# The first 25 microseconds of a chain of eight blocks: statistics of row tiles in another order, one head instead of two corrected on TensorE, other filling products, another buffer

## The chip, the core and the metric

The kernel runs on one core of a Trainium2 chip. The metric is the device time of one execution, in microseconds (us); the number that counts is the median over runs. A core has TensorE (PE in the profile, its weight loads PEld), VectorE (DVE), ScalarE (ACT), GpSimd (POOL) and SyncE (SP), which issues the DMAs here. Each has its own in-order queue of instructions, and they wait for each other by semaphores. Matrix products write to eight banks of PSUM, 128 partitions by 512 numbers each; all else lies in SBUF.

## The reference

x has shape (2, 512, 512): two sequences b of 512 rows, in float32. Eight blocks follow each other, and each adds its result to x:

```
x = x + attn_a(layernorm(x))      # latent attention, 32 heads      <- the change is in here
x = x + ffn(layernorm(x))         # dense layer with adapters
x = x + attn_b(layernorm(x))      # grouped-query attention
x = x + ffn(layernorm(x))
x = x + attn_mla(...); + experts(...); + attn_mha(...); + experts(...)
```

The first block, cut to what matters (`X` is the normalised x, b one sequence):

```
C_q  = X @ Wq_d + bq_d            # 512 x 12
C_kv = X @ Wkv_d + bkv_d          # 512 x 4: keys and, through Wv_u, values of all heads
q    = C_q @ W_qk + b_qk          # 32 heads of width 4
attn = softmax(q_h @ C_kv.T / 2)  # per head
out  = concat_h(attn @ V_h) @ Wo + bo,   V = C_kv @ Wv_u + bv_u
```

## The kernel before, in words

**Tiles.** The 1024 rows of x are eight row tiles t of 128 (`NT` = 4 of each sequence). A layernorm of a tile is `statistics` (three VectorE instructions: L205, L207, and L241 inside `inv_sqrt`, whose power is a GpSimd instruction, L243), then `centred` (L215 on VectorE: subtract the mean, multiply) into one of two buffers "xn", then `place` (four transposes on TensorE, L228, and a ScalarE copy to `xT`, L233).

**High and low halves.** The first block does its score products in the type float32r, whose products are cheap and keep fewer bits. To lose nothing, queries, keys and weights each lie several times along the partitions, some copies as the full number rounded (high) and some as what rounding left over (low). `halved` makes this with two instructions of one engine: `high` = full times a mask (L481), which rounds, and then full plus `high` (L482). The mask of a partition is -1 where the low part is wanted and 0 elsewhere. Its temporary comes from the tag "high", a ring of two buffers.

**A head's queries.** The kernel groups the 32 heads of a sequence into eight products, called `head(b, t)` here, t = 0 to 7 (one 128x512 product each, L503). There are two ways to get their halves:
- by TensorE: ScalarE copies the product to `high` (L506), a second product with `rest` (the masked identity) subtracts it in PSUM (`correct`, L199), and ScalarE copies the result to `qs` (L509). Heads 0 and 1 of the first sequence go this way;
- by GpSimd: ScalarE copies the product to the buffer "wv_diag" (L513; this tag has one buffer), and GpSimd halves it (L481, L482). The others go this way.

**The opening** (L769 to L793) is written out by hand for TensorE and VectorE (`manual_schedule` on both: their instructions keep the order of the code; the order on ScalarE, GpSimd and SyncE is left to the scheduler). `warm(n)` issues n transposes of the identity whose result nobody reads (L86). Then, in order: 30 of these; row tiles 0 to 3 in pairs (statistics of two tiles, centring of the two, and for each tile `place` and 5 or 10 identity products); GpSimd's `fills`, held back behind the last power; the halves of the weights `wqks` (L784, L785); the statistics of row tiles 4 to 7; `queries(0)` (eight product instructions, L473; then L497 and the halves on VectorE) and `latents(0)` (eight more L473; then L490 and the halves, which give `keys`); then heads 0 and 1 side by side, with `fill(2)` after each of three rounds. `fill(n, bank)` issues n products of `unit` (the identity) with `keys[0]`, also read by nobody (L755); unlike those of `warm` they need the keys. The rounds are: both heads' products and L506; both corrections and L509; nothing.

**Twelve steps** follow (L804 to L812). Here only TensorE's order is the code's. Each step has two score products on 32 rows (L589, each read by a VectorE maximum, L597), a slice of other work taken from the list `extra` (`slices(1)`: one piece of cost 1), and `fill(2)`. The list holds, in order: centring of tiles 4 and 5, heads 2 and 3, placements of tiles 4 and 5, centring of 6 and 7, values of the latents (L521, L525), head 4, placements of 6 and 7, heads 5, 6, 7. Eight steps are one unit of scores u; unit u needs head u. After the eighth step the adapters' coefficients are computed on VectorE (L848 to L859), after the ninth `maxima(0)` (four transposes, L615, a correction, L199, and a ScalarE copy, L618) makes the operands of the transposed scores.

**The main loop** has 16 units of eight steps; a step has two scores, two transposed scores (L627, in three banks in turn, each read by an exponent on ScalarE, L630), and a slice of other work or eight value products (L637). The second sequence's projections and heads are done in these slices. Everything behind the first block is scheduled in its own sections, with TensorE's order as written.

**Banks.** From L781 to the main loop, `k.turn()` hands out the banks 3, 4, 5, 7 in turn; scores have 0, 1, 2, and bank 6 takes the filling products.

Of the kernel before, what the change touches and what calls it, by code (L numbers as in the profile page):

```python
# [32 lines left out]
F32R = mybir.dt.float32r  # L33
# [7 lines left out]
NT = S // P  # L41
KC = D // P
NTILES = B * NT
# [385 lines left out]
def attn_latent_small(k, a):  # L429
# [8 lines left out]
    nc, tc = k.nc, k.tc  # L438
    with ExitStack() as ctx:
        lp = ctx.enter_context(tc.tile_pool(name="a", bufs=2))  # L440
# [18 lines left out]
        keys = [one([P, S], f"keys{b}", F32R) for b in range(B)]  # L459
# [4 lines left out]
        def fills():  # L464
            nc.gpsimd.tensor_scalar(rest, k.ident, low[:, 1:2], 1.0, ALU.mult, ALU.mult)
            nc.gpsimd.memset(nm[0], 0.0)
            nc.gpsimd.tensor_copy(unit, k.ident)
            for t in (nm[1], *vals):
                nc.gpsimd.memset(t, 0.0)

        def chained(ps, pairs):
            for i, (lhsT, rhs) in enumerate(pairs):
                nc.tensor.matmul(ps, lhsT, rhs, start=(i == 0), stop=(i == len(pairs) - 1))  # L473
                yield 1

        def halved(engine, out, full, at, tag="high"):

            top = lp.tile(list(out.shape), F32R, tag=tag, name="high")  # L480
            engine.tensor_scalar(top, full, low[:, at : at + 1], 1.0, ALU.mult, ALU.mult)  # L481
            return engine.tensor_tensor(out, full, top.bitcast(F32), ALU.add).ins  # L482

# [2 lines left out]
        def latents(b):  # L486
            ps = k.turn()
            yield from chained(ps, [(wkvd[:, c], k.xT[b][:, c]) for c in range(KC)])
            full = fulls[b] = one([P, S], "full")
            nc.vector.tensor_scalar(full, ps, bkvc, None, ALU.add)  # L490
            k.latest = halved(nc.gpsimd if b else nc.vector, keys[b], full, 0)

        def queries(b):
            ps = k.turn()
            yield from chained(ps, [(wqd[:, c], k.xT[b][:, c]) for c in range(KC)])
            full = one([P, S], "full")
            nc.vector.tensor_scalar(full, ps, bqd, 0.5, ALU.add, ALU.mult)  # L497
            cqs[b] = one([P, S], "cq", F32R)
            halved(nc.gpsimd if b else nc.vector, cqs[b], full, 2)

        def head(b, t):
            ps = k.turn()
            nc.tensor.matmul(ps, wqks[:, t], cqs[b], start=True, stop=True)  # L503
            if (b, t) < (0, 2):
                top = lp.tile([P, S], F32R, tag="high", name="high")
                nc.scalar.copy(top, ps)  # L506
                yield 1
                k.correct(ps, rest, top)
                nc.scalar.copy(qs[b][:, t], ps)  # L509
                yield 0  # L510
                return
            full = one([P, S], "wv_diag")
            nc.scalar.copy(full, ps)  # L513
            halved(nc.gpsimd, qs[b][:, t], full, 1)
            yield 1

        def latent_values(b):

            tp = k.turn()
            for t in range(NT):  # L520
                nc.tensor.transpose(tp[:, bass.ts(t, P)], fulls[b][:, bass.ts(t, P)], k.ident)  # L521
            part = tp.rearrange("p (t d) -> p t d", t=NT)[:, :, 0:5]
            for i in range(4):
                to = vals[b][:, :, i, 5 * i : 5 * i + 5]
                k.latest = nc.vector.tensor_copy(to, part).ins  # L525
            yield 1
# [3 lines left out]
        def centre(*ts, bias=None):  # L530
            for t in ts:
                normal[t] = k.centred(t, bias and bias(), known.pop(t, None))
            yield 0

        def put(t, back=False):
            k.place(t, normal.pop(t), k.turn, back)
            yield 1
# [42 lines left out]
        of_values, other = 6, (7,)  # L580
# [167 lines left out]
        def run(pieces):  # L748
            for piece in pieces:
                for _ in piece:  # L750
                    pass

        def fill(n, bank):
            for _ in range(n):
                nc.tensor.matmul(k.held[:, bank], unit, keys[0], start=True, stop=True)  # L755
# [13 lines left out]
        k.ring = k.EVERY  # L769
        with tc.manual_schedule(engines={mybir.EngineType.PE, mybir.EngineType.DVE}):  # L770
            k.warm(30)
            for t in range(0, NT, 2):
                pair = [k.statistics(t + i) for i in range(2)]
                centred = [k.centred(t + i, known=pair[i]) for i in range(2)]
                for i in range(2):
                    k.place(t + i, centred[i], k.turn)
                    k.warm(5 + 5 * i)
            with tc.issue_after(k.root):
                fills()
                k.masks()  # L780
            k.ring = (3, 4, 5, 7)  # L781
            wqks = k.w.tile([P, 8, P], F32R, tag="w8", name="wqks", bufs=5)
            top = k.w.tile([P, 8, P], F32R, tag="w8", name="high", bufs=5)
            nc.vector.tensor_scalar(top, wqk, low[:, 3:4], 1.0, ALU.mult, ALU.mult)  # L784
            nc.vector.tensor_tensor(wqks, wqk, top.bitcast(F32), ALU.add)  # L785
            known = {t: k.statistics(t) for t in range(NT, NTILES)}
            run([queries(0), latents(0)])
            first = k.latest
            starts = [head(0, t) for t in range(2)]
            for _ in range(3):  # L790
                for piece in starts:
                    next(piece, None)
                fill(2, of_values)  # L793
        extra = [centre(NT, NT + 1), head(0, 2), head(0, 3), put(NT), put(NT + 1)]
        extra += [centre(NT + 2, NT + 3), latent_values(0), head(0, 4), put(NT + 2)]
        extra += [put(NT + 3), head(0, 5), head(0, 6), head(0, 7)]

        later = [queries(1), latents(1)] + [head(1, t) for t in range(4)] + [latent_values(1)]
        later += [fold_bias()] + [head(1, t) for t in range(4, 8)] + [fold()]
        later += [add(t) for t in range(NTILES)]  # L800

        behind = []
        with tc.manual_schedule(engines={mybir.EngineType.PE}):
# [10 lines left out]
            extra = later  # L814
# [871 lines left out]
class Experts:  # L1686
# [111 lines left out]
    def bias(self):  # L1798
        return self.k.load_row(self.a["f1_bias"], D, "bias")
# [370 lines left out]
@with_exitstack  # L2170
def kernel(ctx: ExitStack, tc: tile.TileContext, a: dict, out: bass.AP):
    k = Block(ctx, tc, a["x"], out)
    k.hold()
    block = attn_latent_small(k, a)
    bound = CausalBound(k, a)
    attn_gqa(k, a, bound, block)
    ffn_lora(k, a, block)
    attn_mla(k, a)
    k.release(ctx)
    with k.tc.tile_pool(name="f1", bufs=2) as own:  # L2180
        experts = Experts(k, a, own)
        with k.tc.tile_pool(name="heads", bufs=1) as pool:
            rooms = HeadRooms(k, a, pool)
            experts.first(rooms.fill)
            attn_mha(k, a, bound.register(), rooms, experts)
        experts.end()
# [168 lines left out]
```

## Time and profile before

| | |
|---|---|
| median of three runs | 1966.16 us |
| the three runs | 1965.16 to 1968.29 us |
| the profiled execution: its own time | 1967.16 us |
| its span in the trace | 1965.4 us |
| granted TensorE clock | 0.997 |
| PE, DVE, POOL, ACT busy | 98%, 70%, 52%, 48% of the span |
| instructions of PE | 15610 |

The profile comes from one execution. Line numbers (L503) are those of the code above. In the chain of work that ended last each line is a start, a length and the engine and line that the end hung on at that time. In a timeline each line is a start, a length, an engine, a line, output<-input, sizes and a count; in brackets stands how long the engine was idle before and what ended that. A matrix product's start and end are modelled, so that neighbouring products overlap a little in the timeline, while the chain gives each its own share.

### The profile page before, as it was taken

The numbers are of one execution on the slowest core, as the hardware profiler recorded it, in microseconds if no ns is written. First come the engines' busy times: TensorE is split into PE (matmuls) and PEld (weight loads), VectorE is DVE, ScalarE is ACT, GpSimd is POOL, SyncE is SP. The second block draws the span as 40 slices with busy tenths as digits, with TensorE's granted clock in tenths as the row PEclk, the third lists the DMA queues.
The fourth block names the chain that finished last, engine by engine and source line by source line (L and its number), as shares of the span: only waits on it lengthen the run. The fifth ranks groups of instructions, "written<-read, shape, count | busy, mean of one in ns | idle before, by whom it ended". The sixth has DMA issues, their size and how long they took to land.

```text
span 1965.4 us, 40501 instructions
## 1 busy us (share of the span) xinstructions
PE 1927.3 (98%) x15610; PEld 1198.6 (61%) x15610; DVE 1374.7 (70%) x3457; ACT 938.1 (48%) x2460; POOL 1020.1 (52%) x1112
## 2 busy tenths in 40 slices
PE   9989999999999999999999999999999999999999
PEld 5333356777777777777777545666565554654654
DVE  8889658767776676777775577777677755847853
ACT  3876624444444343444443167666666411641550
POOL 4331055776756667677763246565655546216221
PEclk9999999999999999999999999999999999999999
DMA  3010212323322322232223213020101002002001
GB/s 136 17 44 1 76 66 64 86 73 88 96 67 57 97 77 81 76 98 76 79 79 85 72 22 109 7 74 7 62 13 55 23 12 48 2 3 43 2 2 44
DMA packets 69296, 108.96 MB, mean 55 GB/s; under 512 B 13922, under 2 KB 48994, under 8 KB 62052
## 3 DMA queue, kind: packets, MB, share of 16 engines
q1 hardware_dynamic: 68804, 104.15, 18.2%
q8 instruction: 127, 2.08, 0.4%
q0 software_dynamic: 288, 2.10, 0.3%
q14 instruction: 77, 0.63, 0.1%
HBM read 80.00 MB, written 4.19 MB: 43 GB/s over the span
## 4 chain that ended last, share of the span: by engine, by line
PE 86%; POOL 5%; DVE 5%; issue 3%; ACT 1%; SPq 1%; DMA 0%; POOLq 0%; DVEq 0%; ACTq 0%
PE held L1004 13%; PE held L281 11%; PE held L1139 9%; PE held L190 9%; PE held L357 8%; PE held L637 3%; PE held L589 3%; PE held L1076 3%; PE held L473 2%; PE held L1498 2%; PE sc L190 2%; PE held L1495 1%; PE tp L1771 1%; DVE nm L597 1%; PE held L1496 1%
## 5 line engine op out<-in xcount | busy, mean ns | idle before, releaser
L302 ACT ACTIVATE room<-room,nmax 128x128 f32<-128x128 f32 (+3 forms) x384 | 212.6, 557 | 354.5 <-DVE nmax L292 352.2
L281 PE MATMUL held<-kT,q 128*32 128x32 f32 (+15 forms) x4096 | 263.8, 397 | 5.3 <-DVE invs L310 1.7
L292 DVE CUSTOM_DVE_ANT_0 room<-held,mask 128x128 f32<-128x128 f32 (+3 forms) x384 | 179.1, 488 | 63.3 <-PE held L281 57.7
L281 PEld LDWEIGHTS held<-kT,q 128*32 128x32 f32 x4096 | 143.3, 110 | 87.0 <-issue 37.7
L357 PE MATMUL held<-turned,vals 32*128 32x384 f32 (+7 forms) x2784 | 189.7, 416 | 1.5 <-issue 1.5
L597 DVE TENSOR_REDUCE nm<-held 128x1 f32<-128x512 f32 x256 | 161.6, 683 | 23.3 <-PE held L627 17.9
L357 PEld LDWEIGHTS held<-turned,vals 32*128 32x128 f32 (+1 forms) x2784 | 149.2, 167 | 40.3 <-issue 23.8
L315 ACT ACTIVATE room<-room,invs 128x128 f32<-128x128 f32 (+3 forms) x316 | 153.3, 551 | 41.8 <-DVE invs L310 41.7
L254 DVE TENSOR_TENSOR rows<-rows,held 128x512 f32<-128x512 f32 x198 | 129.5, 673 | 31.9 <-PE held L1004 31.3
L330 DVE STREAM_TRANSPOSE turned<-room 128x1152 f32<-128x1152 f32 x80 | 107.8, 1361 | 40.7 <-ACT room L315 21.6
L243 POOL TENSOR_TENSOR rstd<-ve,mhalf 128x1 f32<-128x1 f32 x64 | 36.3, 569 | 179.2 <-DVE ve L241 176.0
L1165 POOL TENSOR_TENSOR q<-q,room 128x256 f32<-128x256 f32 x64 | 45.2, 728 | 123.7 <-DVE q L1148 113.0
L1183 POOL TENSOR_TENSOR q<-q,cosq 128x512 f32<-128x512 f32 x60 | 88.0, 1467 | 31.6 <-DVE t L1180 31.6
L1139 PE MATMUL held<-room,w 128*128 128x256 f32 x384 | 95.0, 383 | 0.0
L1184 POOL TENSOR_TENSOR q<-q,t 128x512 f32<-128x512 f32 x64 | 86.7, 1355 | 6.3 <-DVE q L1183 2.5
L302 ACT ACTIVATE probs<-probs,nmax 128x128 f32<-128x128 f32 (+3 forms) x128 | 70.6, 553 | 37.4 <-DVE nmax L292 36.6
L589 PEld LDWEIGHTS held<-keys,qs 32*128 32x128 f32 x256 | 30.9, 181 | 94.2 <-DVE nm L597 67.0
L1004 PE MATMUL held<-w,ctxT 128*128 128x256 f32 x360 | 86.5, 383 | 0.1
L630 ACT ACTIVATE pt<-held 128x512 f32<-128x512 f32 x128 | 69.7, 599 | 29.8 <-PE held L627 26.8
L630 ACT ACTIVATE room<-held 128x512 f32<-128x512 f32 x128 | 69.8, 599 | 26.7 <-PE held L627 22.1
L589 PE MATMUL held<-keys,qs 32*128 32x512 f32 x256 | 76.9, 494 | 5.5 <-DVE nm L597 5.2
L2105 POOL TENSOR_SCALAR_AFFINE_SELECT room<-room 128x512 f32<-128x512 f32 x32 | 20.3, 635 | 119.0 <-ACT room L2101 119.0
(439 smaller groups left out, 5011.9 us busy)
## 6 DMA issues: line engine op xcount, KB each, us to landing
w<-in_b_wq SPq DMA_DIRECT2D x16, 1024.0 KB, 4.9
w<-in_b_wo SPq DMA_DIRECT2D x16, 1024.0 KB, 5.3
vals<-v SPq DMA_DIRECT2D x256, 64.0 KB, 2.1
w<-in_m_wo SPq DMA_DIRECT2D x8, 1024.0 KB, 6.6
w<-in_b_wk SPq DMA_DIRECT2D x16, 256.0 KB, 2.7
w<-in_b_wupv SPq DMA_DIRECT2D x16, 256.0 KB, 2.6
w<-in_m_wqn SPq DMA_DIRECT2D x8, 384.0 KB, 3.6
rows<-in_x SPq DMA_DIRECT2D x8, 256.0 KB, 4.2
```

The source lines that it names most:

```text
L190: last = self.nc.tensor.matmul(out, lhsT, rhs, start=(i == 0), stop=(i == len(pairs) - 1))
L254: self.nc.vector.tensor_tensor(x, x, ps.rearrange("p (t d) -> p t d", t=2), op)
L281: nc.tensor.matmul(ps[32 * i : 32 * i + 32, a - lo : b - lo], q[:, at : at + 32], keys[:, a:b], start=True, stop=True,)
L292: nc.vector.tensor_tensor_reduce(out=row, in0=ps[:, :kv], in1=self.mask_back[:, :kv] if qt % 2 else self.mask[:, S - kv :], op0=ALU.add, o ...
L302: nc.scalar.activation(row, row, AF.Exp, bias=nmax, scale=-1.0, accum_out=total[:, qt : qt + 1])
L315: self.nc.scalar.activation(row, row, AF.Identity, scale=each)
L357: self.nc.tensor.matmul(out[:, :, :n], values(i, j), rhs, start=(j == blocks[0]), stop=(j == stop[i]),)
L589: nc.tensor.matmul(ps, qs[b][rows[g], 4 * half + i, bass.ts(qt, P)], keys[b][rows[g]], start=True, stop=True,)
L597: k.latest = nc.vector.tensor_reduce(nm[u % 2][:, qt, at : at + 1], ps, AX.X, ALU.max, negate=True).ins
L630: nc.scalar.activation(probs[u, kc][:, g], ps, AF.Exp)
L1004: k.nc.tensor.matmul(out, lhsT[:, i, bass.ts(t, P)], rhs[i], start=not (after or t or i), stop=i == 1, skip_group_check=True,)
L1139: nc.tensor.matmul(out, lhsT[:, c], rhs[:, c], start=c == 0, stop=c == 1)
```

## The change

- In the order of VectorE, the statistics of tile 2 come before the centring of tile 0, and those of tile 3 between the centrings of 1 and 2. The order on TensorE of placements and identity products stays.
- The statistics of tile 7 come behind `queries(0)` and its halves, ahead of those of `latents(0)`.
- The temporary of the keys' halving of the first sequence is a buffer of the tag "wv_diag" and no longer one of "high".
- Only head 0 is corrected on TensorE in the opening. Head 1 becomes a piece of `extra`, ahead of head 2, and is halved by GpSimd.
- Between head 0's parts stand two times five identity products (`warm`) where there were filling products with the keys; one `fill(2)` remains of three.

```diff
-            top = lp.tile(list(out.shape), F32R, tag=tag, name="high")
+            top = lp.tile(list(out.shape), F32R, tag=tag, name="high", bufs=1 if tag != "high" else None)
...
-            k.latest = halved(nc.gpsimd if b else nc.vector, keys[b], full, 0)
+            k.latest = halved(nc.gpsimd if b else nc.vector, keys[b], full, 0, "high" if b else "wv_diag")
...
-            if (b, t) < (0, 2):
+            if (b, t) == (0, 0):
...
             k.warm(30)
-            for t in range(0, NT, 2):
-                pair = [k.statistics(t + i) for i in range(2)]
-                centred = [k.centred(t + i, known=pair[i]) for i in range(2)]
-                for i in range(2):
-                    k.place(t + i, centred[i], k.turn)
-                    k.warm(5 + 5 * i)
+            ahead = [k.statistics(t) for t in range(3)]
+            centred = [k.centred(t, known=ahead[t]) for t in range(2)]
+            ahead.append(k.statistics(3))
+            for t in range(NT):
+                if t == 2:
+                    centred += [k.centred(i, known=ahead[i]) for i in (2, 3)]
+                k.place(t, centred[t], k.turn)
+                k.warm(10 if t % 2 else 5)
...
-            known = {t: k.statistics(t) for t in range(NT, NTILES)}
-            run([queries(0), latents(0)])
+            known = {t: k.statistics(t) for t in range(NT, NTILES - 1)}
+            run([queries(0)])
+            known[NTILES - 1] = k.statistics(NTILES - 1)
+            run([latents(0)])
             first = k.latest
-            starts = [head(0, t) for t in range(2)]
-            for _ in range(3):
-                for piece in starts:
-                    next(piece, None)
-                fill(2, of_values)
-        extra = [centre(NT, NT + 1), head(0, 2), head(0, 3), put(NT), put(NT + 1)]
+            for _ in head(0, 0):
+                k.warm(5)
+            fill(2, of_values)
+        extra = [centre(NT, NT + 1), head(0, 1), head(0, 2), head(0, 3), put(NT), put(NT + 1)]
```

## The prediction, made before the changed kernel ran

> **What bounds the kernel now.** I read the page's busy shares first: PE is busy for 98% of the span, so the time is the time of TensorE's queue, and an edit counts by how much earlier or later that queue gets through. Then I read the chain that ended last over the stretch which the change touches, the first 45 us (columns: start, length, what):
>
> ```profile
> 10.03 1.08 DVE xn L215
> ...
> 11.16 0.65 PE held L228 x4
> 11.81 1.09 PE held L86 x10
> 12.91 6.88 PE held L473 x16
> 19.82 0.76 DVE full L490
> 20.60 0.50 DVE high L481
> 21.12 0.70 DVE keys L482
> 21.82 0.14 issue
> 21.96 0.70 PE held L755 x2
> 22.66 0.46 PE held L199 x2
> 23.12 0.91 PE held L755 x4
> 24.02 0.43 PE held L589 x2
> ```
>
> The reader is to see three sections: row tiles up to 12.91, two projections (L473) up to 19.8, then the keys' tail on VectorE and, behind it, 2.06 us of PE products (21.96 to 24.02) before the first scores (L589). None of those products but the corrections (L199) computes anything.
>
> Third, the table of busy time by stretches (length, then busy time of PE, weight loads, VectorE, ScalarE, GpSimd):
>
> ```profile
> 19.80:24.00 4.20, 2.48 (x12) 1.47 (x11) 2.85 (x5) 2.25 (x4) 0.00 (x0) 1.00 0.85 302
> 24.00:42.70 18.70, 18.16 (x81) 9.94 (x80) 16.82 (x37) 5.77 (x11) 10.09 (x12) 1.00 0.01 1
> ```
>
> PE is idle only in the first; in the second, VectorE is nearly as full as PE. Last, ScalarE in order of time, at two places:
>
> ```profile
> 21.91 0.59 ACT L506 CAST high<-held 128x512 fp32r<-128x512 f32 x1 [1.27 <-DVE keys L482]
> ...
> 42.94 0.59 ACT L513 COPY wv_diag<-held 128x512 f32<-128x512 f32 x1 [2.19 <-POOL qs L482]
> 43.42 1.10 ACT L630 ACTIVATE room<-held 128x512 f32<-128x512 f32 x2
> ```
>
> The first is head 1's high half waiting for a buffer that the keys' halving reads. The second is a ScalarE copy waiting for GpSimd with the first exponent (L630) right behind it: this is where the gain may be lost again.
>
> **Part 1, statistics of three tiles first.** Nothing is added or taken away: eight tiles' statistics, eight centrings. One tile's statistics are 1.02 us of VectorE (those of tile 0 start at 3.54, those of tile 1 at 4.56). The third tile's now stand before tile 0's centring, so that moves from 5.56 to 6.58, ends at 7.12, and PE's first transposes (L228) start at 7.18 instead of 6.16. The last centring gains: statistics 3 now end near 8.7, its GpSimd power (0.55 to 0.81) near 9.55, so tile 3 is centred by 10.15 (0.55, as the unhindered rows) to 10.65 (1.07, as this one took beside GpSimd's fills), against 11.10. But PE's queue is a list of its own: four placements at 0.59 and 30 identity products at 0.109 (10 in 1.09) are 2.36 + 3.27 = 5.63 us without a gap. 7.18 + 0.06 + 5.63 = 12.87. The projections start at 12.87 instead of 12.91: I take **-0.03 us**. Bounds: if the identity products did not stand in the way, tile 3 at 10.15 plus 0.06 + 0.59 + 1.09 gives 11.9, -1.0; if row tile 2 lands late, tile 0 waits for it. Landings took 2.7 to 4.4 us from issue, tile 2 is issued near 1.7, so 4.4 to 6.1 against a need at 5.58: up to +0.5. The median of the first four, 2.9, says 4.6, in time.
>
> **Part 2, statistics 7 behind the queries' halves.** The queries' L497 waited until 17.01 behind four statistics although its products end near 16.35. It now starts there. Its result is needed by the first head product, behind the keys' products at 19.79, and was ready at 19.0 already: **0**, hidden by L473. The moved statistics (1.02) fit between the queries' halves (end 18.3) and the keys' L490 at 19.8. With that slack of 1.5 gone they would push the keys back by up to 1.02.
>
> **Part 3, head 1 taken out of the opening, another buffer for the keys.** Before: keys at 21.82, then 0.14 issue, 0.70 for two products, 0.46 for two corrections, 0.91 for four products: scores at 24.02. After: head 0's product, five identity products, its correction near 20.66 (head 0's high half ends at 20.63 in this trace and waits for nothing), five identity products, its copy ready near 21.5, all before the keys; then 0.14 + 0.70 and the scores. The corrections (0.46) and four products (0.91) leave the path: **-1.37 us**. The ten identity products are 1.09 us inside the gap in which PE now idles (1.72 before L755): 0. Head 1's L506 wait goes with it. First scores: 24.02 - 0.03 - 1.37 = 22.62. What is late next there is the keys' tail itself (L490 to L482, 1.96 us), unchanged.
>
> A rule to weigh here. The row: the first 30 identity transposes alone ran 15 in the 3.0 us from 1.5 and 17 in the 1.8 us from 4.5, 0.20 against 0.11 us each. The Trainium skill (TensorE: Matmul & The Clock Gate, Part 4: PE-mode transpose) says that transposes do not count as PE work for the clock gate in the way products do; by it the new filling would leave PE looking idle from 19.8 to 21.9, still shorter than the page's window of about 3.4 us (Part 1). By the page's worst reading the next 3.4 us would run at half speed, an estimate of +1.7 us. The row speaks against the reading (transposes alone got the speed up), and I add nothing.
>
> **Part 4, head 1 comes back in the loop.** Twelve steps (two scores, a slice, two filling products), 24.02 to 42.70, 18.68 us. PE's own work there: 12 x (0.43 + 0.46) = 10.68, six heads at 0.43 = 2.58, four placements 2.36, latent values 0.60, maxima 0.68: 16.90; the other 1.78 is waiting for VectorE. The twelfth step had an empty slice; now twelve slices hold seven heads, +0.43. VectorE's work is 24 reductions at 0.62, two centrings 1.00, 0.43 of value copies, 1.71 of adapter coefficients: 18.0, so it is about equally late, and part of the +0.43 falls into PE's waits (38.80 to 41.48 is all VectorE in the chain). Bounds 0 to +0.43; I take **+0.2**, the nearer row being that VectorE stretch in the very last steps. The first step of the main loop then starts at 42.70 - 1.40 + 0.2 = 41.5.
>
> On GpSimd and ScalarE head 1 costs a copy (0.59), L481 (0.70) and L482 (1.27), one more turn of a chain that repeats every 2.76 us (copies at 24.92 and 27.68), since "wv_diag" is one buffer. Heads 1 to 3 end near 31.8 instead of 30.4, head 4 near 34.5, before the split of maxima near 35.3 (36.67 now): no wait. Head 2 is needed only in the main loop.
>
> **Sum.** -0.03 - 1.37 + 0.2 = **-1.2 us**, if nothing later gives it back; from 42.7 on the loop is PE's (56.94 busy of 57.30 up to 100 us) and moves as a whole. The profiled execution took 1967.16 (span 1965.4 and 1.76 around it), so 1965.96 on its own time; it lay 1.0 above the median of 1966.16, and against that median I forecast **1965.0**.
>
> **Rivals.**
>
> *ScalarE's queue gives it back (slower than before).* Heads 5, 6, 7 move one step later each: head 5's product from 36.69 to about 37.5. Their copies go through the single buffer, so head 7's copy ends 0.67 + 5.58 + 0.59 later, at 44.3, while the first exponents are ready near 41.9 now. If they stand behind that copy in ScalarE's queue, the first ends at 44.8 instead of 44.0, and the fourth transposed score of the main loop, which needs the first of three banks, comes at 44.9 against 44.3: +0.5 over before, so -1.2 turns into **+0.5: 1966.7**. It decides as soon as head 7's copy is placed ahead of the first L630. For it: that is the order of the rows above, and the copy waited 2.19 there. Against: at 42.94 the copy was ready before the exponents (43.1), now it is ready 1.4 us after them, and ScalarE's order is not written out by hand; VectorE's centrings at 21.73 ran ahead of reductions that stand before them in the code.
>
> *The rest of the program is ordered anew.* Outside the opening only TensorE has a fixed order. A stall as at 100.11 to 104.70 (copy, GpSimd halves, VectorE, 1.7 us of PE idle in that stretch) may appear or vanish; three of them are 5 us, to **1971** or, vanishing elsewhere as well, **1961**. Nothing in the profile points to either.
>
> *The reordering does nothing at all:* with keys' tail and PE list as they are, parts 1 and 2 give 0 in any case; if part 3's products are only replaced by a wait for head 0's copy (23.45 now), scores start near 23.6: **1965.9**.
>
> **How the numbers follow.** About 0.2% (3.9 us, 1962.2 to 1970.1) is what a measurement of this kernel can tell from no change. Chances: forecast 0.50, ScalarE's queue 0.23, nothing but part of it 0.09: all within it, 0.82. New order for the worse 0.09, for the better 0.09. The range takes the first three, the bounds of part 1 (-1.0, +0.5) and of part 4, and about 1 us by which the three runs shown lie apart on either side: 1962.2 to 1968.2.
>
> **What would show it.** The changed profile should have the first L473 at 12.87, the keys at 21.8, first scores at 22.6, one L506 and no wait of ScalarE for the keys; L513 fifteen times for fourteen. The first L627 near 41.6 says part 4 is right; the order of the last L513 and the first L630 behind 41 us decides between forecast and first rival. I am wrong if the projections start before 12.4 (then the identity products did not bound), if tile 2's landing ends VectorE's wait, or if the difference arises after 100 us.

## The result and the profile after

The changed kernel takes 1972.04 us (median of 22 runs, 1965.50 to 1975.44) against 1966.32 us before (22 runs beside it): a ratio of 1.0028, 95% interval 1.0022 to 1.0034. It is slower by some 5.5 us; 1965.0 had been forecast, with 1968.2 as the upper end.

The profiled execution took 1972.26 us, with a span of 1970.5. Its chain of work that ended last, at the place shown of before and on to the main loop (start, length, what):

```profile
7.11 0.66 PE held L228 x4
...
12.35 6.88 PE held L473 x16
...
20.57 0.70 DVE keys L482
21.27 0.14 issue
21.40 0.70 PE held L755 x2
22.10 0.42 PE held L589 x2
...
41.19 0.70 POOL high L481
41.89 0.07 issue
41.96 1.27 POOL qs L482
43.23 0.02 issue
43.25 0.59 ACT wv_diag L513
43.85 0.04 issue
43.89 0.79 PE held L627
44.68 2.01 PE held L473 x2
46.69 0.72 PE held L589 x2
```

Two things are to be seen. Up to 22.10 the change does more than was forecast: the first scores come 1.92 us earlier than before (24.02); about 0.5 of that lies within what executions differ by (see the run with the statistics alone). But between 41 and 43.9 the chain no longer runs through TensorE. It runs through GpSimd's halves of head 6 and ScalarE's copy of head 7 (L513), and behind them a pair of projection products takes 2.01 us. In the chain of before such a pair (L473 x2, from 43.30) takes 1.05.

TensorE's queue at that point, in order of time (the bracket is the idle time before an instruction and what ended it), and ScalarE's:

```profile
40.59 0.50 PE L589 MATMUL held<-keys,qs 32*128 32x512 f32 x2
41.14 0.49 PE L627 MATMUL held<-qm,keys 32*128 32x512 f32 x1
43.89 0.79 PE L627 MATMUL held<-qm,keys 32*128 32x512 f32 x1 [2.26 <-ACT wv_diag L513]
44.61 2.08 PE L473 MATMUL held<-room,w 128*128 128x512 f32 x2
```

```profile
40.50 0.59 ACT L513 COPY wv_diag<-held 128x512 f32<-128x512 f32 x1 [2.19 <-POOL qs L482]
43.25 0.59 ACT L513 COPY wv_diag<-held 128x512 f32<-128x512 f32 x1 [2.16 <-POOL qs L482]
43.74 0.60 ACT L630 ACTIVATE room<-held 128x512 f32<-128x512 f32 x1
```

The first transposed score (L627) runs on time. The second one waits 2.26 us, and what releases it is the copy of head 7's product. In the kernel before the first two ran together and the projections followed at once:

```profile
42.80 0.50 PE L627 MATMUL held<-qm,keys 32*128 32x512 f32 x2
43.23 1.12 PE L473 MATMUL held<-room,w 128*128 128x512 f32 x2
```

The second score and head 7's product have a PSUM bank in common. The ring of banks 3, 4, 5, 7 is advanced by every turn, and the two calls of `warm` take a turn each. So head 7's product lies in bank 5 now (it lay in bank 3 before), and bank 5 is the second of the transposed scores' three.

How TensorE's clock went meanwhile, in the table of busy time (length, busy time of PE, weight loads, VectorE, ScalarE, GpSimd, then the granted clock, DMA share and rate):

```profile
41.00:42.00 1.00, 0.58 (x3) 0.18 (x1) 0.97 (x3) 0.09 (x1) 0.73 (x2) 1.00 0.00 0
42.00:43.00 1.00, 0.00 (x0) 0.00 (x0) 0.41 (x1) 0.00 (x0) 1.00 (x1) 0.90 0.00 0
43.00:44.00 1.00, 0.11 (x1) 0.11 (x1) 0.00 (x0) 0.75 (x2) 0.28 (x2) 0.50 0.00 0
44.00:50.00 6.00, 6.00 (x13) 1.76 (x13) 1.29 (x2) 2.02 (x4) 1.89 (x2) 0.50 0.00 0
50.00:56.00 6.00, 6.00 (x20) 1.78 (x20) 3.58 (x6) 2.46 (x5) 0.58 (x3) 0.50 0.02 4
56.00:57.00 1.00, 1.00 (x12) 0.03 (x4) 1.00 (x2) 0.80 (x2) 0.92 (x2) 0.77 0.84 250
```

The seventh number of each line falls from 1.00 to 0.50 while TensorE stands idle, and it stays there for 13.65 us (42.80 to 56.46), though TensorE is busy all the time from 43.9 on. In this execution that is most of the loss. At a place in the code that both kernels reach (the first transposition at L655) the profile after is 6.6 us late, 147.6 against 141.0. At the last block's projections it is 4.7 us late (1582.9 against 1578.2), mostly because the execution profiled of before had a half clock of 3.4 us near 1160 us that this one did not have; it accounts for 1.7 of the 1.9 us between the two.

**Taking the clock apart from the waits.** Every run lists its mean granted clock. Time x (1 - clock) is how much of TensorE's clock was withheld, and the rest of the time is a figure for the program at full clock. It is a reckoning and not a measurement of its own: it also counts clock that is withheld while TensorE waits (in the profile after, 42.80 to 43.89), so it puts a little of a wait down to the clock. Averaged over the runs:

| kernel | median, us | ratio to before, 95% | withheld clock, us | at full clock, us |
|---|---|---|---|---|
| before (35 runs beside the first four) | 1966.35 | | 5.2 | 1960.8 |
| changed | 1972.04 | 1.0028 (1.0022 to 1.0034) | 9.3 | 1962.35 |
| warm products in bank 6 | 1968.60 | 1.0016 (1.0007 to 1.0026) | 8.2 | 1961.0 |
| ten filling products more | 1968.69 | 1.0014 (1.0005 to 1.0023) | 6.2 | 1962.2 |
| heads 5 and 6 earlier | 1969.05 | 1.0017 (1.0007 to 1.0027) | 8.9 | 1960.4 |
| before, statistics alone | 1966.25 | 0.9999 (0.9990 to 1.0008) | 5.1 | 1960.9 |
| changed, copies in buffers of their own | 1964.40 | 0.9990 (0.9981 to 0.9999) | 5.9 | 1958.4 |
| changed, two heads on TensorE | 1965.77 | 0.9996 (0.9987 to 1.0005) | 6.4 | 1959.45 |
| before, head 7 in bank 5 | 1967.03 | 1.0000 (0.9992 to 1.0009) | 4.5 | 1961.6 |
| changed, no warm products | 1973.53 | 1.0040 (1.0025 to 1.0055) | 12.6 | 1960.9 |
| before, copies in buffers of their own | 1963.92 | 0.9990 (0.9981 to 0.9999) | 3.9 | 1960.1 |
| as the copies' one, no warm products | 1966.55 | 1.0001 (0.9990 to 1.0013) | 8.2 | 1958.1 |

The runs were taken in three groups, each with runs of before beside it, to which its ratios refer: rows 3 to 6 (before as in the first row), rows 7 to 10 (before 1966.50, 5.8 withheld, 1960.7 at full clock) and the last two (1965.08, 4.9, 1960.8). The changed kernel's ratio refers to the 22 runs of before beside it, whose clocks are not on record. The standard errors of the last two columns are 0.1 to 0.4 at full clock and 0.3 to 0.7 for the clock (1.2 and 1.7 in the two runs without warm products). The changed kernel's 5.6 us over the first row, by these means, are 4.1 of clock and 1.5 of waits.

### The profile page after: what moved, and what is told of

Same layout as the page of the kernel before. It is cut to its first block, busy times and chain, and to the rows that moved or that the text cites. A ratio compares the mean times of both kernels' runs of the same rounds, so it can differ in the third digit from the quotient of the medians.

```text
span 1970.5 us, 40514 instructions
## 1 busy us (share of the span) xinstructions
PE 1932.3 (98%) x15615; PEld 1199.2 (61%) x15615; DVE 1374.8 (70%) x3457; ACT 937.2 (48%) x2459; POOL 1023.5 (52%) x1114
## 4 chain that ended last, share of the span: by engine, by line
PE 87%; POOL 5%; DVE 5%; issue 2%; ACT 1%; DMA 0%; SPq 0%; DVEq 0%; POOLq 0%; ACTq 0%
PE held L1006 13%; PE held L281 11%; PE held L1141 9%; PE held L190 9%; PE held L357 8%; PE held L637 3%; PE held L589 3%; PE held L1078 3%; PE held L473 2%; PE sc L190 2%; PE held L1500 2%; PE held L1497 1%; PE pj L190 1%; PE tp L1773 1%; PE held L1498 1%
## 5 line engine op out<-in xcount | busy, mean ns | idle before, releaser
L315 ACT ACTIVATE room<-room,invs 128x128 f32<-128x128 f32 (+3 forms) x316 | 153.3, 551 | 41.6 <-DVE invs L310 41.5
```

The source lines that it names most:

```text
L315: self.nc.scalar.activation(row, row, AF.Identity, scale=each)
```

## The experiments

**Theory A:** head 7's late copy holds the bank of the second transposed score; TensorE idles, and the idle time costs it the clock. **Rival B:** the exponents behind that copy in ScalarE's queue are the cause, whatever the bank. **Rival C:** the opening's new order costs the clock by itself.

**The identity products in bank 6, no turn of the ring.**

```diff
-                k.warm(5)
+                k.warm(5, k.held[:, of_values])
```

> The ten identity products between head 0's parts write to bank 6 and take no turn of the ring 3, 4, 5, 7; the order of every engine's instructions stays that of the changed kernel. Head 7's product then lies in bank 3 instead of 5. Theory A (bank 5 is the second transposed score's bank, so this product waits 2.26 us for ScalarE's copy of head 7, and the idle TensorE loses its clock): the second transposed score follows the first near 41.4 instead of 43.89; only the third waits, about 0.9 us to 43.85, and the fourth about 0.4 us for the first exponent; the clock stays full; time within 0.7 us of before, 1966 to 1967. Rival B (the exponents behind head 7's copy in ScalarE's queue are the cause, banks do not matter): clock halves as in the changed kernel, 1971 to 1973. Rival C (the half clock has to do with the opening's other order, not with that idle time): 1971 to 1973 as well.

Measured: 1968.60, ratio 1.0016 (1.0007 to 1.0026), above the range of A and below that of B and C. At full clock it is 1961.0, within 0.2 of before, as A said: the bank accounts for 1.3 us of waiting. But 3.0 us of clock stay lost. In its trace the first two transposed scores run together at 42.86, and the next two wait:

```profile
42.86 0.50 PE L627 MATMUL held<-qm,keys 32*128 32x512 f32 x2
...
45.53 0.59 ACT L513 COPY wv_diag<-held 128x512 f32<-128x512 f32 x1 [2.17 <-POOL qs L482]
46.01 2.07 ACT L630 ACTIVATE room<-held 128x512 f32<-128x512 f32 x4
...
46.17 0.99 PE L627 MATMUL held<-qm,keys 32*128 32x512 f32 x2 [1.21 <-ACT wv_diag L513]
```

So the bank decides where the wait falls, and not that there is one. Head 7's copy is late in either case, and it still stands ahead of the first exponent, which is rival B's place. A needs this amendment: the cause is the late copy, and the bank made it worse. This profile does not show the 3.0 us being lost at that wait: its only half clock near the place lay ahead of it, from 35.8 to 39.2, and delayed the whole stretch. The run without identity products (below) has the same ring and no such spell: there the first two ran together at 40.94, the next two waited 1.20 us for the same copy, to 44.25, and the clock halved at 44.58.

**Ten filling products more, ahead of the main loop.**

```diff
             run(extra)
+            fill(10, of_values)
             extra = later
```

> The changed kernel with ten more filling products (10 x 0.23 us) between the twelve steps and the main loop, so that TensorE is busy while it would have waited for bank 5. Theory A: the second transposed score still comes near 43.9, 1.1 us later than in the kernel before, but the clock stays full: about 1.0 us over before, 1967 to 1968, so 4 to 5 us less than the changed kernel although it does 2.3 us more. Rival C (the idle time does not set the clock): 1972 or, with the added products in the way, up to 1974.

Measured: 1968.69, 3.4 us less than the changed kernel for ten more products that nobody reads. The second transposed score came at 44.52 (0.57 us of idle time before it), and the granted clock was 1.00 throughout that stretch:

```profile
40.50:44.50 4.00, 3.44 (x16) 2.34 (x15) 1.71 (x3) 1.21 (x3) 2.54 (x3) 1.00 0.00 0
44.50:58.00 13.50, 13.48 (x70) 4.72 (x74) 10.40 (x18) 9.15 (x18) 4.34 (x6) 1.00 0.06 21
```

The withheld clock falls from 9.3 to 6.2 us, against 5.2 of before, and the time at full clock stays (1962.2 against 1962.35). C falls with it: the opening is the same, and filling the idle time gives most of the clock back. The median lies 0.7 above the range given.

**Heads 5 and 6 earlier in the list.**

```diff
-        extra += [centre(NT + 2, NT + 3), latent_values(0), head(0, 4), put(NT + 2)]
-        extra += [put(NT + 3), head(0, 5), head(0, 6), head(0, 7)]
+        extra += [centre(NT + 2, NT + 3), latent_values(0), head(0, 4), head(0, 5)]
+        extra += [put(NT + 2), head(0, 6), put(NT + 3), head(0, 7)]
```

> The changed kernel with heads 5 and 6 one place and two places earlier in the list, ahead of the placements of tiles 6 and 7, so that GpSimd's chain of 2.76 us per head ends earlier. Head 7's copy should end near 41.0 instead of 43.84, ahead of the second transposed score at 41.5. Theory A: no wait, full clock, the 1.9 us that the first scores gained are kept to within 0.3: 1964.2 to 1965. Rival B: the same, since the exponents are not held up either; it tells A and B from C (1971 to 1973) and is the version that should beat both kernels.

Measured: 1969.05. A miss for both theories, and head 7's copy ended at 44.44 and not near 41.0. No exponent waited for it, but the wait had moved: GpSimd took head 5's halves ahead of the split of the maxima (L606, L607), and `maxima(0)` (L615) waited for that. The chain of this run:

```profile
35.95 1.26 POOL qs L482
37.22 0.15 POOL top L606
37.37 0.07 issue
37.44 0.24 POOL nm L607
37.68 0.04 issue
37.72 0.66 PE held L615 x4
```

The granted clock fell there as well (0.71 from 40 to 45 us). With one buffer for the copies, an earlier place for one head delays other work of GpSimd.

**The statistics alone, on the kernel before** (the hunks of the diff on `ahead`, `centred` and `known`; the rest as before).

> The kernel before with the statistics alone in the new order (tiles 2 and 3 ahead, tile 7 behind the queries). The projections start at 12.35 as in the changed kernel, 0.56 earlier than before, and nothing later is touched: theory A expects 0.4 to 0.6 us less than before, 1965.8. Rival C would have some of the 5 us here: 1968 or more.

Measured: 1966.25, ratio 0.9999 (0.9990 to 1.0008). The projections do start early in its trace, at 12.46, but the 0.5 us can't be told from nothing in the time. The profiles of the other runs say why. In the nine that have the new order, the projections start between 12.35 and 13.28; in five of them the chain runs through the landing of row tile 2, the case that the prediction priced at up to +0.5. In the three that have the old order they start at 12.38, 12.86 and 12.91. So the 0.56 us between the two profiles compared is within what one execution differs from another. None of the loss shows here.

**ScalarE's copies in two buffers of their own.**

```diff
-            full = one([P, S], "wv_diag")
+            full = lp.tile([P, S], F32, tag="copied", name="copied")
             nc.scalar.copy(full, ps)
```

> The changed kernel, but ScalarE's copies of the heads' products go to a tag of two buffers of their own instead of the one buffer wv_diag, so that a copy no longer waits for GpSimd's halving of the head before it. Theory A, as the first four runs left it (head 7's copy, held up by the chain of 2.76 us per head, is what the second transposed score and the first exponents wait for; the waits cost some 1.5 us at full clock and some 4 us in lost clock): head 6's and head 7's copies run near 38.9 and 41, the second transposed score near 41.5 without a wait; at full clock 1.5 to 1.9 us under before, the clock's losses as in before: 1964.2 to 1965.2. Rival B' (the opening's order itself costs clock, whatever the wait): 1968 to 1970, as in the runs with the bank or the heads changed.

Measured: 1964.40, ratio 0.9990 (0.9981 to 0.9999): 7.6 us under the changed kernel by the medians, with the same instructions in the same order on TensorE. Head 7's copy starts at 40.58 instead of 43.25, the exponents follow at once, and the second transposed score comes 0.5 us behind the first, as the copy ends, where it came 2.75 behind:

```profile
40.69 1.03 PE L627 MATMUL held<-qm,keys 32*128 32x512 f32 x2
41.65 1.13 PE L473 MATMUL held<-room,w 128*128 128x512 f32 x2
```

```profile
40.58 0.59 ACT L513 COPY copied<-held 128x512 f32<-128x512 f32 x1 [0.92 <-POOL qs L482]
41.28 1.09 ACT L630 ACTIVATE room<-held 128x512 f32<-128x512 f32 x2
```

This is the run that settles it. Nothing in the opening was undone, the seven heads are still GpSimd's, and head 7 still lies in bank 5. Only the copies' wait for GpSimd is shorter (0.92 us at head 7 instead of 2.16), and all of the loss is gone. At full clock the kernel is 2.4 us under before; how much of that is the change's own, and how much the buffers', the run of before with the same buffers tells (below).

**Two heads corrected on TensorE again, the rest of the change kept.**

```diff
-            if (b, t) == (0, 0):
+            if (b, t) < (0, 2):
...
+            starts = [head(0, t) for t in range(2)]
+            for _ in range(2):
+                for piece in starts:
+                    next(piece, None)
+                k.warm(5, k.held[:, of_values])
```

> The changed kernel with one part undone: heads 0 and 1 are both corrected on TensorE in the opening, so GpSimd has six heads and the list starts with head 2, as before; identity products in bank 6. The new statistics order, the keys' other buffer and one fill of two products stay. Theory A: first scores near 22.1 as in the changed kernel, GpSimd's chain one head shorter, head 7's copy near 42 and the third transposed score near 42.4 hardly held up: 1.3 to 1.9 us under before at full clock, 1964.4 to 1965.2. Rival B': 1968 or more, since the opening up to the scores is the changed kernel's. If it is fast, the part of the change that costs is the head moved to GpSimd.

Measured: 1965.77, ratio 0.9996 (0.9987 to 1.0005); 1.3 under before at full clock, as expected of A; the median 0.6 above the range. No transposed score waits in its profile. The run to compare it with is the one in bank 6, which has the same ring of banks and differs by head 1 alone: it takes 1.6 us more at full clock (1961.0) and has 1.8 more of the clock withheld (8.2 against 6.4). So the head moved to GpSimd is the part of the change that costs. The first scores came at 23.05, later than expected, because row tile 2 landed late in this execution and everything behind it moved (the chain: start, length, what):

```profile
1.72 4.68 DMA rows<-in_x
...
13.28 6.87 PE held L473 x16
...
23.05 0.42 PE held L589
```

From the start of the projections to the first scores are 9.77 us, against 9.75 in the changed kernel and 11.11 before. So correcting head 1 on TensorE costs the opening nothing that shows; what shortened it lies in the rest of part 3 of the prediction.

**The kernel before with head 7 in bank 5** (the ring advanced by two turns, nothing else).

```diff
+            k.turns = (k.turns + 2) % 4
```

> The kernel before with the ring of banks advanced by two turns ahead of the twelve steps, nothing else: head 7's product then lies in bank 5, as in the changed kernel. There its copy ends near 43.5 and the second transposed score comes at 42.95. Theory A: a wait of about 0.6 us, the clock rarely lost: 1966.5 to 1967.5. A theory that the bank by itself costs the 5 us (whenever head 7 is made): 1970 to 1972.

Measured: 1967.03, ratio 1.0000 (0.9992 to 1.0009). The second transposed score does wait:

```profile
42.80 0.50 PE L627 MATMUL held<-qm,keys 32*128 32x512 f32 x1
43.58 0.50 PE L627 MATMUL held<-qm,keys 32*128 32x512 f32 x1 [0.28 <-ACT wv_diag L513]
```

By the averages that is 0.9 us more at full clock than the runs beside it and no clock lost by it (4.5 withheld against 5.8). The bank by itself does not cost the 5 us; it does little while head 7 is made in time.

**The changed kernel without the identity products between head 0's parts.**

```diff
             for _ in head(0, 0):
-                k.warm(5)
+                pass
```

> The changed kernel without the ten identity products between head 0's parts; the ring of banks is then that of the kernel before, as in the run with the products in bank 6, to which it is compared (1968.6). TensorE idles about 2 us before the keys. If the identity products keep the clock, this loses more of it: 1969.5 to 1971. If they are worth nothing: 1968 to 1969.2.

Measured: 1973.53, ratio 1.0040 (1.0025 to 1.0055), the slowest of all and 2.5 above the upper range. It is to be compared with the run in bank 6, since the ring is the same: the same time at full clock (1960.9 against 1961.0), and 12.6 us of clock withheld against 8.2. The standard errors are 1.7 and 0.6, so the difference of 4.4 is 2.4 of its own errors. The profile (of a run of 1968.81, the second fastest of eight) does not show where: TensorE stood idle 0.77 and 0.71 us ahead of the keys and kept its clock there, and the half clock came at the main loop's wait, from 44.6 to 54.8.

**The same two edits the other way.** The copies' buffers on the kernel before, and the identity products taken out of the fastest variant of the changed kernel.

> The kernel before with ScalarE's copies of the heads' products in two buffers of their own, as in the fastest run so far (the changed kernel with that edit: 1964.4, 2.3 us under before at full clock). If the gain of that run is the change's earlier scores, set free by the buffers, this one gains little: the first exponent is 0.3 us earlier, 1965.8 to 1966.6. If it is the buffers' own gain, 1964 to 1965.

Measured: 1963.92, ratio 0.9990 (0.9981 to 0.9999). By median that is the outcome named for "the buffers' own gain", a little under its range. At full clock it gains 0.7 us, of which about 0.3 was expected; the rest of the lower median is clock, 3.9 withheld against 4.9 of the runs beside it, which is within the errors. Against this kernel the fast variant of the change is 1.7 us shorter at full clock (1958.4 against 1960.1), but not by median (1964.40 against 1963.92), because it has 2.0 us more of the clock withheld (errors 0.6 and 0.7); of these, 0.9 also lie between the runs of before in the two groups (5.8 against 4.9). Against the runs of before beside them both have the ratio 0.9990. So the change's own gain, with the buffers in both kernels, is 1.7 us by the reckoning at full clock and is not shown in the time.

> The changed kernel with the copies in two buffers of their own and without the ten identity products between head 0's parts. If those products keep the clock in general, clock is lost here too: 1967 to 1971. If they matter only when a wait follows, or not at all, as the run with the buffers: 1963.6 to 1965.2.

Measured: 1966.55, ratio 1.0001 (0.9990 to 1.0013), between the two ranges: 0.3 less at full clock than with the identity products, and 8.2 us of clock withheld against 5.9, a difference of 2.3 with an error of 1.3. The profile (of the slowest run, 1970.85) shows one place. TensorE was idle for most of the time before the keys, the clock fell 1.0 us after it had work again, and it was back 13.65 us later, with no other wait near:

```profile
19.20:21.40 2.20, 0.81 (x3) 0.19 (x1) 1.98 (x4) 1.17 (x2) 0.36 (x1) 1.00 0.99 409
21.40:22.50 1.10, 1.00 (x4) 0.48 (x4) 0.87 (x2) 0.00 (x0) 0.00 (x0) 0.99 1.04 400
22.50:36.00 13.50, 13.50 (x38) 7.66 (x37) 7.63 (x12) 2.93 (x5) 5.90 (x6) 0.50 0.10 30
```

Both pairs of runs point the same way: the identity products are worth something on the clock, some 2 to 4 us with errors of 1.3 and 1.8, and nothing otherwise.

## Why the prediction was wrong, point by point

- **Part 1, -0.03.** The projections began at 12.35, 0.56 earlier than before and ahead of the 12.4 that the prediction gave as a sign that the identity products did not bound. They did: TensorE's list is without a gap from 7.11 to 12.35. A size was wrong: the placements behind the first take 0.44 in an unbroken queue, and 0.59 had been read from the twelve steps. The other sign, row tile 2's landing, did appear in five of the nine profiles with this order; VectorE waits 0.97 us for it in the run with two heads. By itself the part is worth nothing that shows.
- **Part 2, 0.** Right; L473 hides it.
- **Part 3, -1.37, first scores at 22.62.** They came at 22.10, by part 1's error. Right in size: from the projections' start to the first scores are 9.75 us instead of 11.11, 1.36 less. But the run with two heads on TensorE has this too, so moving head 1 was not needed for it. The ten identity products were costed at nothing, which is right for the queue; without them some 2 to 4 us of clock are lost.
- **Part 4, +0.2, main loop's first scores at 41.5.** They began at 40.59 and the first transposed score at 41.14, so nothing had been lost up to there. From the first scores on the twelve steps took 18.56 us, against 18.68 before (PE's queue, 22.03 to 40.59 and 23.95 to 42.63): the +0.2 did not show.
- **The step that failed** is the sum's condition, "if nothing later gives it back", with the loop that "moves as a whole". The loop did move as a whole, but not from its first scores on: head 1 on GpSimd and the earlier scores together bring its transposed scores well ahead of head 7's copy (41.14 against 43.25; before, 42.80 against 42.94), which hangs on a chain of 2.76 us per head and doesn't move with TensorE. The first rival named this copy, its wait and its end (44.3; measured 43.84), gave it 0.23 and a price of +0.5. Two things were missing in it. The ring was not followed to its end: with two turns taken by `warm`, the second transposed score waits where the fourth had been expected to. And the idle time was priced at its own length; the sum had no term for the clock, which was the greater price: 13.65 us of half speed in the profile. By the means over all runs the waits cost 1.5 us over before where 1.2 less had been forecast, and the clock cost another 4.1.
- **The rule weighed under part 3** was set aside for a reason that the runs bear out on average: with ten transposes of the identity less clock is withheld. What deserved weight was the other rule cited, that of the Trainium skill (TensorE: Matmul & The Clock Gate, Part 1) by which the clock falls after about 3.4 us of idle time. Here it fell 1.2 us after the last product had ended, in a gap of 2.26 us. The measurement decides: a gap well below that figure can cost the clock. It need not: the gap of 1.72 us ahead of the keys kept its clock in all four profiles that have it (before, statistics alone, head 7 in bank 5, before with the copies' buffers).
- **The new order of the rest of the program** played no part that shows. From the first transposition at L655 to the last block's projections the profile after takes 1435.3 us (147.6 to 1582.9) and the one before 1437.2 (141.0 to 1578.2), 1.7 of which are its half clock near 1160.

What stays open: whether a given gap costs the clock differs from run to run (the changed kernel's runs lie between 1965.50 and 1975.44), and no run here shows what sets it. One thing that the traces show may bear on it: in each of the twelve, all changes of the clock lie whole multiples of 3.41 us behind its first rise, which comes anywhere from 4.30 to 7.41 us after the start, so the same gap falls on this grid differently each time. Idle time alone does not decide: the 3.41 us ahead of the fall at 42.80 hold 1.2 us of it, those ahead of a fall at 1677.6 in the run in bank 6 none, and before has 1.5 us near 1407 without a fall. The clock's own share in the two runs without identity products is known to 1 or 2 us only.

## What to carry to other kernels

When an edit brings one engine's work forward, look for what can't follow: here a chain of copies through one buffer that paces itself by another engine; a second buffer for it turned a loss of 5.5 us into a gain of 2. Price a wait of TensorE by the clock that it may lose as well as by its length, and read the granted clock next to each gap. Follow a ring of buffers through every call that takes a turn, useless work included.

## What the runs showed of the hardware that was not expected

The half clock came in pieces of 3.41 us (in the run in bank 6, 35.8 to 39.2) or of two, three or four times that: 6.8 (1805.1 to 1812.0 with two heads on TensorE), 10.2 (44.6 to 54.8 without identity products) and 13.65 (42.80 to 56.46 in the changed kernel, 22.5 to 36.1 with the copies' buffers and without identity products). TensorE was busy nearly all through these, but for the first 1.1 us of the one at 42.80. In the kernel before, over 87 runs beside the experiments, 4.9 to 5.8 us of clock per execution are withheld on average, in a few places; the time at full clock differs much less from run to run (standard deviation 0.7 us) than the time (1.9 us).
